# Nine of sixteen transpositions of normalized tokens move from TensorE to VectorE in an attention and mixture-of-experts kernel

## The chip, the cores and the metric

The kernel runs on one core of one Trainium2 chip. A core has engines that each run their own stream of instructions in order: TensorE (PE in the profile, with its weight loads as PEld), VectorE (DVE), ScalarE (ACT), GpSimd (POOL), and SyncE (SP), which here only issues DMAs. They work on SBUF, an on-chip memory of 128 partitions. TensorE writes its results into PSUM, a second one, of eight banks of 128 partitions x 512 f32. The metric is the device time of one execution in microseconds.

## The reference

The input x is 4096 tokens of 256 f32. One layer of a transformer is computed, all in f32:

```python
n = layernorm(x)                       # no scale, no shift
Q, K, V = n @ Qw, n @ Kw, n @ Vw
x = x + softmax(mask(Q @ K.T / 16)) @ V            # causal, one head of 256
h = layernorm(x) @ W_in + b_in
probs = softmax(h @ W_gate + b_gate)   # 8 experts
topv, topi = top_k(probs, 2); topv = topv / sum(topv)
out_e = relu(h @ W1[e] + b1[e]) @ W2[e] + b2[e]    # 256 -> 1024 -> 256
x = x + (sum over the two chosen e of topv_e * out_e) @ W_out + b_out
```

Each token goes through two of the eight experts, and only those are computed.

## The kernel before, in words

**Tokens.** The 4096 tokens are 8 blocks b of 512 (`TB`), a block is 4 tiles of 128. The whole x lies in SBUF (`xb[b]`), tokens on partitions. TensorE contracts over partitions, so whatever is multiplied by a weight matrix must first be turned, features on partitions. That is wanted twice for each block, sixteen times in all: for the first layer norm (k=0, the turned block `zT[b]` serves as keys and gives queries and values) and for the second (k=1, `z1T`, input of the experts). `ln_stats` (L214) takes mean and variance of a tile on VectorE, `ln_rstd` (L219) makes the reciprocal root of a block on GpSimd, `ln_rows` (L225) makes the shift (L229) and normalizes four tiles on VectorE (L236). `turn` (L242) turns a block: eight 128x128 transposes on TensorE into two PSUM tiles of tag `tr` (L247), each copied to SBUF by VectorE (L248).

**Attention.** It goes by half blocks of 256 queries, g = 0 to 15, with b = g // 2 and q = g % 2. `scores(g)` makes the scores transposed, keys on partitions, one piece of 256 keys x 256 queries at a time, c = 0 to g: eight matmul instructions into one of four PSUM banks of tag `mm` (L453), a copy to SBUF by ScalarE (L462) and then, on VectorE, a running elementwise maximum over the pieces (L468, "mx"). The last piece is masked (L472). The maxima are brought together in `top` (L480 to L483), turned by TensorE (`pt`, L489), reduced, and spread over all partitions (`pmax`, L496). VectorE subtracts them from every piece (L500, L506), and ScalarE takes the exponential (L503, L509). Pieces lie in 24 SBUF buffers of tag `s`. `attend(g)` multiplies the pieces by the values (`po`, L518), divides by the sum, adds to x (L528, L530) and takes the second norm's statistics. `project(b)` makes queries and values of a block (L411, L423). Qw and Kw are first multiplied into one matrix, so that the normalized tokens themselves serve as keys.

**Order.** The loop over g (L950) writes scores(g+1) ahead of attend(g). In a half g with q = 0 it normalizes block b+1 for the first norm, runs `enter(b-1)` (turn of the second norm, `ph` matmuls for h and the router, two DMAs to `rows` in DRAM on SP's queue, L275), turns block b+1, attends, projects block b+1, and runs `route(b-1)` (top two experts and each token's place, some thirty small VectorE operations, eight indirect stores to `slots` on GpSimd's queue, L341, and x += b_out on GpSimd, L360). In a half with q = 1 it ends with `ln_rstd(1, b)`, the first norm's statistics of block b+2, and the second norm's normalization of block b. In the last block's first half (g = 14) `enter(6)` is called in the middle of scores(15), at c = `BETWEEN`; then come `plan("a")`, the table of the experts' full blocks made from the first six token blocks, `route(6)`, and the first four `fetch_rows` (a slot list on SP's queue, L691, and two indirect gathers from `rows` on GpSimd's queue, L707) and three `fetch_weights` (SP's queue).

What is written in this order isn't yet the order of execution. A planner of the kernel framework runs the program ahead of time with its own prices for each instruction, and lets each engine take, of what is ready in that run, what stands first in the program. The order found so is then fixed for each engine's stream; semaphores keep it correct on the chip whatever the true durations are. Tiles of one tag share a set number of buffers, and a tile waits until a buffer is free. `tc.keep_in_program_order(ins)` adds an edge from the instruction that was written just before `ins` on the same engine, so the planner can't take `ins` ahead of it; the expert phase uses it through `pin` (L769).

**Experts.** From L1065 on, blocks of 256 or 128 token slots run through their expert: rows gathered, turned by VectorE in 32x32 squares (`squares`, L773, `STREAM_TRANSPOSE`), two matmul layers (L812 or L842, L879), results scattered to `parts`. At the end the two parts of each token are added (L1010), turned and multiplied by W_out.

Of the kernel before, what the change touches and what calls it, by code (L numbers as in the profile page):

```python
# [29 lines left out]
USUAL = 6  # L30
BETWEEN = 6
KT = VT = 8
# [3 lines left out]
def preln_attention_moe_kernel(  # L36
# [50 lines left out]
    stream = ctx.enter_context(tc.tile_pool(name="stream", bufs=1))  # L87
    dram = ctx.enter_context(tc.tile_pool(name="dram", bufs=1, space=bass.MemoryType.DRAM))
    psum = ctx.enter_context(tc.tile_pool(name="psum", bufs=1, space=bass.MemoryType.PSUM))

# [18 lines left out]

    def load_square(w, name, queue=nc.sync):  # L110
        t = const.tile([P, ND, w.shape[1]], F32, tag=name, name=name)
        queue.dma_start(out=t, in_=w.rearrange("(c p) e -> p c e", p=P))
        return t

    def load_row(v, name):
# [3 lines left out]


    kw_sb = load_square(Kw, "kw", nc.scalar)
    qw_sb = load_square(Qw, "qw", nc.scalar)
    for j in range(TPB):
# [100 lines left out]

    def ln_rows(k, b, pool):  # L225

        s = ts(b, TPB)
        mv, rstd, shift = lns[k]
        nc.vector.scalar_tensor_tensor(  # L229
            shift[:, s, :], mv[:, s, 0:1], -1.0, rstd[:, s, :], ALU.mult, ALU.mult  # L230
        )
        zs = []
        for j in range(TPB):
            t = b * TPB + j
            z = pool.tile([P, D], F32, tag=f"z{k}", name=f"z{k}_{t}", bufs=TPB)
            nc.vector.tensor_scalar(  # L236
                z, xb[b][:, j, :], rstd[:, t, :], shift[:, t, :], ALU.mult, ALU.add
            )
            zs.append(z)
        return zs  # L240

    def turn(k, b, zs, zT):  # L242

        for c in range(ND):
            pt = ps_tr(f"pz{k}_{b}_{c}")
            for j in range(TPB):
                nc.tensor.transpose(pt[:, ts(j, P)], zs[j][:, ts(c, P)], ident)  # L247
            nc.vector.tensor_copy(zT[:, c, :], pt)  # L248


# [3 lines left out]

    def enter(b, zs, pool):

        zT = pool.tile([P, ND, TB], F32, tag="z1T", name=f"z1T{b}", bufs=1)
        turn(1, b, zs, zT)
        hr = pool.tile([P, TPB, D], F32, tag="hr", name=f"hr{b}", bufs=1)

        lg = pool.tile([P, TPB, NE], F32, tag="lg", name=f"lg{b}", bufs=2)
        for j in range(TPB):
            ph = ps_mm(f"ph{b}_{j}")
            for c in range(ND):
                nc.tensor.matmul(
                    ph[:, :DG],
                    lhsT=zT[:, c, ts(j, P)],
                    rhs=win_sb[:, c, :],
                    start=(c == 0),
                    stop=(c == ND - 1),  # L270
                )
            nc.vector.tensor_tensor(lg[:, j, :], ph[:, D:DG], bgate_bc, ALU.add)
            nc.vector.tensor_tensor(hr[:, j, :], ph[:, :D], bin_bc, ALU.add)
        for k in range(TOPK):
            put = nc.sync.dma_start(  # L275
                out=rows[ts(b, TOPK * TB), :].rearrange("(t p k) d -> p t k d", p=P, k=TOPK)[
                    :, :, k, :
                ],
                in_=hr,
            )  # L280
            if b == NB - 1:
                tc.add_to_no_dep_group("last", put.ins)

        return lg
# [80 lines left out]

    attn = ctx.enter_context(tc.tile_pool(name="attn", bufs=1))

# [10 lines left out]
    def prepare_scores():  # L378

        wT = {}  # L380
        for name, w in (("qwT", qw_sb), ("kwT", kw_sb)):
            wT[name] = attn.tile([P, ND, D], F32, tag=name, name=name)
            pt = ps_tr(f"p{name}")
# [52 lines left out]

    def scores(g, between=None):


        b, q = divmod(g, QPB)  # L440
        ss, mx = [], None
        top = attn.tile([P, QB], F32, tag="top", name=f"top{g}", bufs=2)
        for c in range(g + 1):
            if between is not None and c == BETWEEN:
                between()
            ps = ps_mm(f"ps{g}_{c}")
# [14 lines left out]
            if c < g:  # L461
# [3 lines left out]
                else:  # L465
                    old = mx
                    mx = attn.tile([P, TB], F32, tag="mx", name=f"mx{g}_{c}", bufs=2)
                    nc.vector.tensor_tensor(mx, ps, old, ALU.max)  # L468
                continue
# [249 lines left out]
    def fetch_weights(item, homes=None):  # L719
        nonlocal used  # L720
        k, m = item
        parties = sets_of(item)
        sets, c2 = [], attn.tile([P, D], F32, tag="z0", name=f"c2_{k}{m}", bufs=TPB)
        es = [
# [48 lines left out]
    def squares(to, of):  # L773


        for f in range(P // SQ):
            for q in range(P // SQ):
                pin(
                    nc.vector.transpose(  # L779
                        to[ts(f, SQ)][..., ts(q, SQ)], of[ts(q, SQ)][..., ts(f, SQ)]  # L780
                    )
                )

    def turn_rows(item, h):
# [3 lines left out]
        hT = piece(f"hT_{k}{m}", ND, su * P)  # L788
        squares(
            hT.rearrange("p c (u s) -> p c u s", u=su),  # L790
            h.rearrange("p u (c f) -> p c u f", c=ND),
        )
        return hT
# [114 lines left out]
    ready = prepare_scores()  # L908
    first_rows = ln_rows(0, 0, attn)
    with tc.issue_after(ready.ins):  # L910
# [12 lines left out]
    for e in range(NE):  # L923
# [19 lines left out]
    nc.sync.dma_start(  # L943
        out=rows[TOPK * (S - TB) :, :].rearrange("(t p) d -> p t d", p=P),
        in_=zero.unsqueeze(1).to_broadcast([P, TOPK * (TPB + 1), D]),
    )

    prepare_biases()
    row = scores(0)
    for g in range(NT // KU):  # L950
        b, q = divmod(g, QPB)
        coming = q == 0 and b + 1 < NB
        lg = []

        def send():
            lg.append(enter(b - 1, rows1, attn))


        last = q == 0 and b == NB - 1
        nxt = None  # L960
        if g + 1 < NT // KU:
            nxt = scores(g + 1, send if last else None)
        if coming:
            ahead = ln_rows(0, b + 1, attn)
        if last:

            early = seen
            tables["a"] = plan("a", early, NFULL, SB, 0)
            seen = route(b - 1, lg[0], seen, attn)
            got, hTs = {}, {}  # L970
            for n in range(AHEAD + 1):
                got[n] = fetch_rows(work[n])
            for n in range(AHEAD):
                got[n] += fetch_weights(work[n])
            weighed = AHEAD
        elif q == 0 and b > 0:
            send()
        if coming:
            turn(0, b + 1, ahead, zT[b + 1])
        attend(g, row)  # L980
        row = nxt
        if coming:
            project(b + 1)
        if lg and not last:
            seen = route(b - 1, lg[0], seen, attn)
        if q == QPB - 1:
            ln_rstd(1, b)
            if b + 2 < NB:
                stats0(b + 2)
            rows1 = ln_rows(1, b, attn)  # L990

# [76 lines left out]
    for n, item in enumerate(work):  # L1068
# [21 lines left out]
        if n == 0:  # L1090
            lg = enter(NB - 1, rows1, attn)
        if n == 1:
# [70 lines left out]
```

## Time and profile before

| what | value |
|---|---|
| median of 10 runs | 1093.93 us (1093.12 to 1094.18) |
| the profiled execution | 1093.2 us, span 1091.3 us |
| TensorE busy | 1074.1 us, 98% of the span |
| VectorE busy | 692.1 us, 63% |
| ScalarE, GpSimd busy | 330.9 us, 236.9 us |
| granted TensorE clock | 1.0 throughout |
| attention ends, expert phase begins | at about 586 us |

Times are microseconds from the span's start unless ns is written. A line of a group has source line, engine, operation, output<-inputs by tile names, shapes and count, then busy time, mean duration of one in ns, idle time of the engine just before them and what ended it. A line of the timeline has start, length, engine, line, operation, and in brackets the engine's idle time before it with what released it. Matmuls are pipelined: the duration of one is longer than the distance to the next, so that costs on TensorE are read from distances between starts, not from the mean duration. An f32 matmul shows as two matmul instructions, an f32 transpose as one.

### The profile page before, as it was taken

The numbers are of one execution on the slowest core, as the hardware profiler recorded it, in microseconds if no ns is written. First come the engines' busy times: TensorE is split into PE (matmuls) and PEld (weight loads), VectorE is DVE, ScalarE is ACT, GpSimd is POOL, SyncE is SP. The second block draws the span as 40 slices with busy tenths as digits, with TensorE's granted clock in tenths as the row PEclk, the third lists the DMA queues.
The fourth block names the chain that finished last, engine by engine and source line by source line (L and its number), as shares of the span: only waits on it lengthen the run. The fifth ranks groups of instructions, "written<-read, shape, count | busy, mean of one in ns | idle before, by whom it ended". The sixth has DMA issues, their size and how long they took to land. (4 is left out here: it accounts for less than half of the span.)

```text
span 1091.3 us, 15704 instructions
## 1 busy us (share of the span) xinstructions
PE 1074.1 (98%) x5067; PEld 891.6 (82%) x5067; DVE 692.1 (63%) x2134; ACT 330.9 (30%) x727; POOL 236.9 (22%) x286
## 2 busy tenths in 40 slices
PE   7999999999999999999999999999999999999998
PEld 5768888888888888888888888786868777777887
DVE  5678576574574555446392753858678876767636
ACT  1223233332341423223132122232322332323244
POOL 2023211212001110201222332223232231313110
PEclk9999999999999999999999999999999999999999
DMA  8010101001001000100074466787979796969285
GB/s 268 1 39 1 39 2 38 2 1 40 1 1 39 1 1 1 39 1 25 16 261 160 136 189 211 252 302 245 318 237 329 242 342 209 337 216 320 92 290 192
DMA packets 114888, 148.34 MB, mean 136 GB/s; under 512 B 23149, under 2 KB 94770, under 8 KB 114804
## 3 DMA queue, kind: packets, MB, share of 16 engines
q1 hardware_dynamic: 105876, 129.70, 35.9%
q0 software_dynamic: 8384, 17.09, 4.8%
q8 instruction: 41, 0.67, 0.3%
q14 instruction: 43, 0.35, 0.2%
q10 hardware_dynamic: 544, 0.52, 0.1%
HBM read 124.79 MB, written 22.75 MB: 135 GB/s over the span
## 5 line engine op out<-in xcount | busy, mean ns | idle before, releaser
L518 PE MATMUL po<-v,s 128*128 128x257 f32 x1056 | 238.3, 380 | 0.7 <-ACT s L509 0.7
L453 PE MATMUL ps<-qT,zT 128*128 128x256 f32 x1088 | 232.8, 374 | 0.0
L453 PEld LDWEIGHTS ps<-qT,zT 128*128 128x128 f32 x1088 | 202.9, 190 | 27.1
L518 PEld LDWEIGHTS po<-v,s 128*128 128x128 f32 x1056 | 196.9, 190 | 27.7 <-issue 1.6
L462 ACT COPY s<-ps 128x512 f32<-128x512 f32 x120 | 70.2, 585 | 193.4 <-PE ps L453 154.3
L879 PE MATMUL pe_a<-w_a,mid_a 128*128 128x256 f32 x544 | 121.3, 380 | 0.0
L812 PE MATMUL pm_a<-hT_a,w_a 128*128 128x256 f32 x544 | 120.0, 379 | 0.0
L341 POOL DMA_INDIRECT slots<-assign,ati x64 | 62.6, 978 | 259.8 <-DVE ati L339 238.1
L468 DVE TENSOR_TENSOR mx<-ps,mx 128x512 f32<-128x512 f32 x91 | 62.8, 690 | 88.5 <-ACT s L462 88.0
L879 PEld LDWEIGHTS pe_a<-w_a,mid_a 128*128 128x128 f32 x544 | 102.7, 190 | 19.0 <-issue 5.6
L812 PEld LDWEIGHTS pm_a<-hT_a,w_a 128*128 128x128 f32 x544 | 103.4, 190 | 14.1
L821 ACT ACTIVATE mid_a<-pm_a,c_a 128x256 f32<-128x256 f32 x136 | 64.2, 472 | 165.6 <-PE pm_a L812 150.9
L503 ACT ACTIVATE s<-s 128x512 f32<-128x512 f32 x120 | 71.7, 629 | 51.4 <-DVE s L500 50.9
L779 DVE STREAM_TRANSPOSE hT_a<-h_a 32x128 f32<-32x128 f32 x272 | 82.2, 302 | 3.7
L500 DVE TENSOR_TENSOR s<-s,pmax 128x512 f32<-128x512 f32 x120 | 73.0, 679 | 8.2 <-PE pmax L496 8.2
L888 POOL DMA_INDIRECT parts<-y_a,slot_a x34 | 34.1, 1004 | 161.7 <-DVE y_a L887 150.8
L779 DVE STREAM_TRANSPOSE mid_c<-raw_c 32x256 f32<-32x256 f32 x128 | 55.8, 436 | 1.9
L879 PE MATMUL pe_b<-w_b,mid_b 128*128 128x256 f32 x256 | 56.8, 380 | 0.0
L812 PE MATMUL pm_b<-hT_b,w_b 128*128 128x256 f32 x256 | 56.6, 379 | 0.0
L879 PEld LDWEIGHTS pe_b<-w_b,mid_b 128*128 128x128 f32 x256 | 48.5, 190 | 9.4 <-issue 2.6
L812 PEld LDWEIGHTS pm_b<-hT_b,w_b 128*128 128x128 f32 x256 | 48.6, 190 | 6.6
L821 ACT ACTIVATE mid_b<-pm_b,c_b 128x256 f32<-128x256 f32 x64 | 30.1, 470 | 63.0 <-PE pm_b L812 63.0
(276 smaller groups left out, 1200.3 us busy)
## 6 DMA issues: line engine op xcount, KB each, us to landing
w_a<-in_L_ffn_W_dram SPq DMA_DIRECT2D x68, 512.0 KB, 5.7
w_d<-in_L_ffn_W_dram SPq DMA_DIRECT2D x48, 512.0 KB, 6.8
w_c<-in_L_ffn_W_dram SPq DMA_DIRECT2D x32, 512.0 KB, 7.9
w_b<-in_L_ffn_W_dram SPq DMA_DIRECT2D x32, 512.0 KB, 6.6
rows<-hr SPq DMA_DIRECT2D x16, 512.0 KB, 3.0
yp<-parts SPq DMA_DIRECT2D x14, 512.0 KB, 8.9
x<-in_L_attn_x_dram SPq DMA_DIRECT2D x7, 512.0 KB, 7.0
out_dram<-ot SPq DMA_DIRECT2D x14, 256.0 KB, 6.0
```

Source lines behind the costliest of these rows:

```text
L341: put = nc.gpsimd.indirect_dma_start(out=slots, out_offset=bass.IndirectOffsetOnAxis(ap=ati[:, j : j + 1], axis=0), in_=assign[:, b * TPB ...
L453: nc.tensor.matmul(ps[:, u * QB + lo : (u + 1) * QB], lhsT=zT[kt // TPB][:, d, ts(kt % TPB, P)], rhs=qT[b][:, d, q * QB + lo : (q + 1) * Q ...
L462: nc.scalar.copy(flat, ps)
L468: nc.vector.tensor_tensor(mx, ps, old, ALU.max)
L500: nc.vector.tensor_tensor(s, s, pm[:, :QB].unsqueeze(1).to_broadcast([P, KU, QB]), ALU.subtract)
L503: nc.scalar.activation(s, s, AF.Exp)
L518: nc.tensor.matmul(po[u][:, : D + 1], lhsT=ss[c][:, k, ts(u, P)], rhs=vb[kt // TPB][:, kt % TPB, :], start=(kt == 0), stop=(kt == g * KU + u),
L779: nc.vector.transpose(to[ts(f, SQ)][..., ts(q, SQ)], of[ts(q, SQ)][..., ts(f, SQ)])
L812: nc.tensor.matmul(pm[:, :SB], lhsT=w1[c][:, ts(f, P)], rhs=hT[:, c, :], start=(c == 0), stop=(c == ND - 1),)
L821: nc.scalar.activation(mid[f // 2][:, f % 2, :], pm[:, :SB], AF.Relu, bias=c1[:, f : f + 1])
L879: nc.tensor.matmul(pe[ts(j, rest), :D], lhsT=mid[f][:, ts(u, P)][:, ts(j, rest)], rhs=w2[f // (NF // 2)][:, f % (NF // 2), :], start=(f == 0),
L888: put = nc.gpsimd.indirect_dma_start(out=parts, out_offset=bass.IndirectOffsetOnAxis(ap=slot[:, u : u + 1], axis=0), in_=y[:, u, :], in_of ...
```

## The change

`TURNED = (4, 2)` takes the place of `BETWEEN = 6`. Blocks from 4 on of the first norm (4, 5, 6, 7) and blocks 2 to 6 of the second are no longer turned by TensorE but by VectorE, nine of sixteen. For such a block `ln_rows` returns its work as a list (`fill`) in place of doing it: one shift, four normalizations, and from `rows_todo` sixteen transposes, each of 32 partitions x 256 elements. The next call of `scores` takes the list, and puts equal parts of it behind its running maxima c = 1 to g-1, each instruction tied to the one before by `keep_in_program_order`. So the first norm's block b+2 is turned in scores(2b+2), g = 6, 8, 10, 12, and the second norm's block b in scores(2b+3), g = 7, 9, 11, 13, 15.

To that end the first norm's statistics and normalization of block b+2 move from the end of half q = 1 to the end of half q = 0, behind `route`, for all blocks. `enter` no longer turns. In half g = 14 `enter(6)` leaves the middle of scores(15); the table and the four `fetch_rows` come ahead of it and `route(6)` behind attend(14). Since rows are then fetched before blocks 6 and 7 have entered, the zeros that are stored in `rows` at the start reach over both blocks. The four normalized tiles of a block are one tile with one buffer (`z0`, `z1`), and Kw, Qw, their turned copies and later the rows of b2 share one tag (`sq`) with four buffers.

```diff
-BETWEEN = 6
+TURNED = (4, 2)
+    def square(name):
+        return attn.tile([P, ND, D], F32, tag="sq", name=name, bufs=4)
-    def ln_rows(k, b, pool):
+    def ln_rows(k, b, fill=None):
...
+        todo = [shifts] + [partial(normalize, j) for j in range(TPB)]
+        if fill is None:
+            for do in todo:
+                do()
+        else:
+            fill += todo
+        return z
+    def squares_todo(to, of):
+        return [
+            partial(nc.vector.transpose, to[ts(f, SQ)][..., ts(q, SQ)], of[ts(q, SQ)][..., ts(f, SQ)])
+            for f in range(P // SQ)
+            for q in range(P // SQ)
+        ]
+    def rows_todo(hT, h):
+        return squares_todo(
+            hT.rearrange("p c (u s) -> p c u s", s=P), h.rearrange("p u (c f) -> p c u f", f=P)
+        )
-    def scores(g, between=None):
+    def scores(g, fill=()):
+        parts_of = max(g - 1, 1)
...
-                    nc.vector.tensor_tensor(mx, ps, old, ALU.max)
+                    done = nc.vector.tensor_tensor(mx, ps, old, ALU.max)
+                    for do in fill[len(fill) * (c - 1) // parts_of : len(fill) * c // parts_of]:
+                        tc.keep_in_program_order(done)
+                        done = do()
+                    if fill:
+                        tc.keep_in_program_order(done)
...
-        out=rows[TOPK * (S - TB) :, :].rearrange("(t p) d -> p t d", p=P),
-        in_=zero.unsqueeze(1).to_broadcast([P, TOPK * (TPB + 1), D]),
+        out=rows[TOPK * (S - LATE * TB) :, :].rearrange("(t p) d -> p t d", p=P),
+        in_=zero.unsqueeze(1).to_broadcast([P, TOPK * (LATE * TPB + 1), D]),
...
     row = scores(0)
+    ahead = ln_rows(0, 1)
+    fill = []
     for g in range(NT // KU):
...
-            nxt = scores(g + 1, send if last else None)
+            nxt = scores(g + 1, fill)
+        fill = []
+        if q == 0:
+            if b == NB - 1:
+                early = seen
+                tables["a"] = plan("a", early, NFULL, SB, 0)
+                got, hTs = {}, {}
+                for n in range(AHEAD + 1):
+                    got[n] = fetch_rows(work[n])
+            if b > 0:
+                if b - 1 < TURNED[1]:
+                    turn(1, b - 1, rows1, z1T)
+                lg = enter(b - 1, z1T, attn)
+            if b == NB - 1:
+                for n in range(AHEAD):
+                    got[n] += fetch_weights(work[n])
+                weighed = AHEAD
+            elif b + 1 < TURNED[0]:
+                turn(0, b + 1, ahead, zT[b + 1])
         attend(g, row)
         row = nxt
-        if coming:
+        if q == 0 and b + 1 < NB:
             project(b + 1)
-        if lg and not last:
-            seen = route(b - 1, lg[0], seen, attn)
+        if lg is not None:
+            seen = route(b - 1, lg, seen, attn)
+        if q == 0 and b + 2 < NB:
+            stats0(b + 2)
+            by_dve = b + 2 >= TURNED[0]
+            ahead = ln_rows(0, b + 2, fill if by_dve else None)
+            if by_dve:
+                fill += rows_todo(zT[b + 2], ahead)
         if q == QPB - 1:
             ln_rstd(1, b)
-            if b + 2 < NB:
-                stats0(b + 2)
-            rows1 = ln_rows(1, b, attn)
+            z1T = attn.tile([P, ND, TB], F32, tag="z1T", name=f"z1T{b}", bufs=1)
+            by_dve = TURNED[1] <= b < NB - 1
+            rows1 = ln_rows(1, b, fill if by_dve else None)
+            if by_dve:
+                fill += rows_todo(z1T, rows1)
```

## The prediction

> **What bounds the kernel now.** First the page: engine totals, then the slices.
>
> ```profile
> PE 1074.1 (98%) x5067; PEld 891.6 (82%) x5067; DVE 692.1 (63%) x2134; ACT 330.9 (30%) x727; POOL 236.9 (22%) x286
> DVE  5678576574574555446392753858678876767636
> ```
>
> TensorE is busy 98% of the span, so time is gained only by taking work from it, and lost by any hole put into it. VectorE has room, unevenly. Then busy time by stretch (columns PE, PEld, DVE, ACT, POOL) tells where TensorE still idles:
>
> ```profile
> 27.00:64.00 37.00, 32.48 (x159) 25.80 (x157) 26.56 (x76) 10.78 (x27) 5.02 (x5) 1.00 0.00 1
> 64.00:124.00 60.00, 59.23 (x279) 48.01 (x276) 45.12 (x155) 15.56 (x35) 12.95 (x13) 1.00 0.11 36
> 124.00:184.00 60.00, 60.00 (x286) 50.86 (x286) 40.30 (x118) 18.61 (x37) 12.81 (x13) 1.00 0.06 18
> 443.00:586.00 143.00, 142.71 (x667) 122.87 (x666) 75.13 (x218) 37.56 (x69) 26.86 (x27) 1.00 0.22 72
> ```
>
> From 124 us on there is no hole. Each new one is paid in full. Next the groups, for prices:
>
> ```profile
> L247 PE MATMUL pz<-ident,z 128*128 128x128 f32 x128 | 17.8, 273 | 1.8 <-DVE s L506 1.8
> L248 DVE COPY z1T<-pz 128x512 f32<-128x512 f32 x16 | 10.9, 686 | 14.6 <-PE pz L247 14.4
> L779 DVE STREAM_TRANSPOSE hT_a<-h_a 32x128 f32<-32x128 f32 x272 | 82.2, 302 | 3.7
> L779 DVE STREAM_TRANSPOSE mid_c<-raw_c 32x256 f32<-32x256 f32 x128 | 55.8, 436 | 1.9
> ```
>
> Last the timeline around scores(6) (124.07 to 139), with two earlier lines where TensorE waited for VectorE:
>
> ```profile
> 59.04 0.33 PE L489 MATMUL pt<-ident,top 128*128 128x128 f32 x1 [1.51 <-DVE top L481]
> 104.12 0.65 PE L489 MATMUL pt<-ident,top 128*128 128x128 f32 x2 [0.42 <-DVE top L481]
> 114.21 1.04 PE L247 MATMUL pz<-ident,z 128*128 128x128 f32 x8
> 115.08 1.90 PE L518 MATMUL po<-v,s 128*128 128x257 f32 x8
> 124.07 11.91 PE L453 MATMUL ps<-qT,zT 128*128 128x256 f32 x56
> 137.56 0.42 PE L489 MATMUL pt<-ident,top 128*128 128x128 f32 x2
> ```
> ```profile
> 56.38 2.00 DVE L480 TENSOR_TENSOR top<-mx 128x256 f32<-128x256 f32 x1
> 130.19 0.69 DVE L468 TENSOR_TENSOR mx<-ps,mx 128x512 f32<-128x512 f32 x1 [1.08 <-ACT s L462]
> 136.85 0.41 DVE L481 TENSOR_TENSOR top<-top,s 128x256 f32<-128x256 f32 x1
> 609.42 4.40 DVE L779 STREAM_TRANSPOSE hT_a<-h_a 32x128 f32<-32x128 f32 x14
> 613.85 0.42 DVE L887 TENSOR_TENSOR y_a<-pe_a,c_a 128x256 f32<-128x256 f32 x1
> ```
>
> A score piece takes TensorE 1.73 us (eight matmuls, 216 ns apart); VectorE spends 0.69 on its maximum and idles about 1.04. That hole is what the change fills. The top of scores(6) is there at 136.85+0.41 = 137.26 and its turn pt starts at 137.56: the fixed order meets the maxima with 0.3 us to spare. Where VectorE was later than planned, TensorE stood (1.51 and 0.42).
>
> **What the change takes from TensorE.** A turn's eight transposes run from 114.21 to 115.08, 0.87 us (109 ns each; the 273 of the group is overlapping duration). Nine turns: **-7.8 us**, all on the path. Here a rule of the Trainium skill speaks against the change: "VectorE: DVE Perf Modes", sections "The three transpose paths" and "Rules for kernel authors", advises TensorE for a whole 128x128 turn and prices it at 390 ns there. By its figure the nine turns would free 72 x 0.39 = 28 us, an estimate from that page for another data type; the trace's 109 ns stands.
>
> **What it gives VectorE.** Off: 18 copies of 0.686, 12 us. On: 144 transposes of 32x256, 436 ns long, which follow one another about 14 ns apart (in the 32x128 row, 4.40/14 = 314 against 302): 0.45 each, 65 us. A fill is 16 x 0.45 = 7.2, plus the shift (0.2) and four normalizations (0.345 apart) that move in: 8.8 us over g-1 parts in scores(g), g = 6 to 13 and 15. Per part: 1.76 (g=6), 1.46, 1.25, 1.10, 0.97 (g=10), down to 0.63. From g=10 it fits the 1.04 hole. For g = 6 to 9 the maxima slip by 0.72, 0.42, 0.21, 0.06 a part, at most 2.9 us at the last maximum. TensorE may run ahead of a maximum by four banks: 3 x 1.73 less copy and maximum (0.585+0.69) leaves 3.9 us, so the slip alone doesn't stop it. Behind the last maximum, its part and the 1.2 us chain to top (136.02 to 137.26) are late too; attend(g-1) is there to fill that, 10.4 us at g=6, if the order places it. The edges themselves add one wait: a fill's first maximum stands behind the last VectorE instruction of the iteration before, a statistic that is out by then; 0. Behind a fill item that waits stand all later maxima, the masks and top, and behind these, by banks or by pt, TensorE.
>
> **Does the order know?** The order is fixed by a planner with its own prices, and the trace shows one being low. Expert block 0 puts out y_a at 609.08 and 613.85; the second is released by 16 matmuls after the first, 16 x 0.217 = 3.47 us, and comes earlier in the program than the transposes. On the chip 7 of these fit before it; the planner put 14. So it counts at most (3.47-0.42)/13 = 0.235 for what takes 0.314. With the 134 ns that 128 more elements cost (436-302), a 32x256 is planned at 0.37 or less against 0.45. Then pt, or for the second norm the first ph, is placed too early. At 0.37 the lateness that isn't planned is 16 x 0.08 = 1.25 us for g = 6, 7, 8, where VectorE is the slower one at either price, 0.94 for 9, where holes take up some of it, and only the last part's, 0.26 or less, from 10 on. Less the 0.3 to spare: 3 x 0.95 + 0.64 = **+3.5**. Ends: 0 if the planner's price is right; 6.8 (same working) if it plans 0.30, what the shorter 32x128 takes. I take 3.5, the value that the order of y_a gives.
>
> **The collisions with GpSimd.** x<-x,bout (2.35 us) held the SBUF-to-SBUF maximum at 56.38 for 2.00 us where its kind takes 0.53, and cost the 1.51 above. In the blocks that TensorE still turns, the first norm's shift and normalizations leave scores(3) and scores(5), where both waits were, for the project before; the collision stays. Between 0 and -1.9: **-0.7**. In the fills of the second norm it can hold a shift or normalization 2 us; only g=7 and 9 have no hole for it. Between 0 and +4: **+0.5**, since GpSimd is free for it right after rstd and mostly done when the pinned shift comes.
>
> **The rest.** Waits of pq and ph for turned copies go: 0 to -0.9, **-0.3**. stats0(b+2) and its two GpSimd operations move ahead of the second half of block b; their price is in the rival below. Merged z tiles and kw, qw, turned weights and b2 rows sharing one tag: the same number of slots, and turn(0,b+1) ends long before the next normalization; 0. The zero store grows from 10 to 18 tiles of 128 KB, 1.05 MB, 4 us of DMA at the 268 GB/s of the first slice; behind it on SP's queue the next store is hr at 68 us; 0. At the end of attention four slot loads on SP and eight gathers (1.26 us apart, 10 us of GpSimd) go ahead of block 6's enter and route; its two row stores then wait for the gathers on SP's queue, weights queue behind these, and its eight slot stores come 25 us later. The cover is attend(14) and attend(15), 54 us of TensorE; weights now leave at 546 and are first used at 586. If that cover were short, lateness would be paid up to some 2 us; enter(6) in the middle of scores(15) costs no hole to undo (0.3 idle in 443 to 586): **0**.
>
> Sum: -7.8+3.5-0.7+0.5-0.3 = **-4.8 us** on the profiled execution: 1093.2 (span 1091.3) becomes 1088.4. The runs' median, 1093.93, is 0.7 above it: **1089.1**.
>
> **Rivals.**
> *All hidden.* The planner's price is right for this shape, or TensorE arrives later than I think: -8.8, 1085.1. For it: no wait for pt from 124 us on. Against it: the 14 transposes ahead of y_a.
> *Given back whole.* Planned price of 0.27 to 0.30 and one or two collisions: 6 to 10 us back, 1091.7 to 1096, no measurable change. For it: the 0.235 is an upper bound. Against it: VectorE idles whole microseconds elsewhere.
> *Slower: the shift behind the slot stores.* rstd of the next first norm must now pass GpSimd near route's eight slot stores. In block 2 they start at 125.40; behind them rstd would end 8 x 1.26 + 1.3 later, 136.8, while the pinned shift is due at 129.1 and every maximum stands behind it. 7.7 late less 3.9 of banks leaves 3.8 us of TensorE for each of four fills, 15 us: 1104. It decides from about 6 us late a fill. For it: statistics come last in the program. Against: attend's statistics already interleave with route's small operations, which leaves them done by about 124.
>
> **How the numbers follow.** What this kernel's measurement tells from no change is about 0.2%, 2.2 us. The forecast (2 to 6 given back, 1086.5 to 1091.5) 0.45; all hidden 0.20; given back whole 0.19; slower 0.16. Faster 0.65, same 0.19, slower 0.16. The range goes from the all-hidden end, 1085, to 1097: it leaves out the far part of the slower case and a sliver below.
>
> **What would show it.** L247 down to 56 transposes and a new 32x256 transpose group of 144 near 436 ns; TensorE's busy share unchanged; waits of pt or ph for VectorE of about a microsecond at scores(6) to (9), few later. Wrong if TensorE shows holes inside the score pieces (banks), if shift waits for rstd on GpSimd, or if pt doesn't wait at all.

## The result and the profile after

| | before | after |
|---|---|---|
| median | 1093.91 us | 1103.49 us (8 runs, 1100.52 to 1104.14) |
| ratio | | 1.0085, interval 1.0076 to 1.0094 |
| profiled execution, span | 1093.2, 1091.3 us | 1102.56, 1100.8 us |
| TensorE busy, idle within the span | 1074.1, 17.2 us | 1072.6, 28.2 us |

The change costs 9.6 us; 4.8 us of gain were forecast. The page of the changed kernel, engine totals and TensorE's row of slices:

```profile
PE 1072.6 (97%) x4995; PEld 887.4 (81%) x4995; DVE 734.1 (67%) x2260; ACT 331.3 (30%) x727; POOL 236.8 (22%) x286
...
PE   7999999999999999999989999999999999999998
```

VectorE has 42 us more: the turns less the dropped copies make 50.4, and five shifts of the first norm give 9.6 back. Before, these five took 2.08 us each, from 97.38 to 99.47 us for one, while GpSimd's x += b_out ran from 97.09 to 99.44; now every shift of the first norm takes 0.15 or 0.16. TensorE's totals hardly move, and one slice of its row falls from 9 to 8. The busy time by stretch (columns PE, PEld, DVE, ACT, POOL, granted clock, DMA share, GB/s) says where it now idles:

```profile
27.00:64.00 37.00, 33.69 (x163) 26.71 (x162) 26.82 (x76) 11.39 (x27) 4.89 (x5) 1.00 0.03 5
...
124.00:184.00 60.00, 55.46 (x249) 46.56 (x248) 48.16 (x138) 17.22 (x33) 11.44 (x11) 0.97 0.06 18
184.00:256.00 72.00, 69.16 (x324) 59.20 (x323) 53.29 (x145) 23.19 (x45) 12.79 (x13) 1.00 0.05 15
...
443.00:586.00 143.00, 138.83 (x635) 118.46 (x634) 81.52 (x232) 37.66 (x69) 26.98 (x27) 0.99 0.23 58
```

Where TensorE had been busy for 60.00 of 60, it is busy for 55.46; in the stretch at the end of attention 4.2 us are idle, where 0.3 were. The clock, 1.00 everywhere before, is 0.97 and 0.99 in two of these rows. The groups, shapes kept apart, show that the change itself did what it says:

```profile
L495 DVE STREAM_TRANSPOSE z1T<-z 32x256 f32<-32x256 f32 x80 | 34.9, 436 | 1.7
L495 DVE STREAM_TRANSPOSE zT<-z 32x256 f32<-32x256 f32 x64 | 27.9, 436 | 1.3
...
L261 PE MATMUL pz<-ident,z 128*128 128x128 f32 x56 | 8.5, 291 | 1.0 <-DVE s L535 1.0
```

144 turns of 436 ns on VectorE, 56 transposes left on TensorE. Counted from start to start, the transposes take 9.0 us of TensorE's time in place of 16.4. The list of TensorE's waits (total, times, longest) names three that are new or grown; before, pt had 1.9 us, ph 0.2, and pk was not listed:

```profile
PE pt L518 <- DVE top L510: 5.5, 4, 2.2
PE ph L290 <- DVE z1T L495: 4.5, 5, 2.4
PE pk L348 <- DVE both L339: 4.2, 2, 3.9
```

The first two are one kind, seen in the timeline of scores(6), VectorE and then TensorE, and in that of scores(7):

```profile
128.00 0.69 DVE L492 TENSOR_TENSOR mx<-ps,s 128x512 f32<-128x512 f32 x1 [3.21 <-ACT s L486]
...
130.91 1.32 DVE L495 STREAM_TRANSPOSE zT<-z 32x256 f32<-32x256 f32 x3
...
135.52 1.79 DVE L495 STREAM_TRANSPOSE zT<-z 32x256 f32<-32x256 f32 x4
137.34 0.69 DVE L492 TENSOR_TENSOR mx<-ps,mx 128x512 f32<-128x512 f32 x1
138.07 2.25 DVE L495 STREAM_TRANSPOSE zT<-z 32x256 f32<-32x256 f32 x5
...
141.18 0.42 DVE L510 TENSOR_TENSOR top<-top,s 128x256 f32<-128x256 f32 x1
```
```profile
123.64 11.91 PE L477 MATMUL ps<-qT,zT 128*128 128x256 f32 x56
135.39 4.07 PE L547 MATMUL po<-v,s 128*128 128x257 f32 x18
141.65 0.66 PE L518 MATMUL pt<-ident,top 128*128 128x128 f32 x2 [2.18 <-DVE top L510]
...
167.77 1.57 PE L290 MATMUL ph<-win,z1T 128*128 128x264 f32 x6 [2.36 <-DVE z1T L495]
```

VectorE idles for 3.21 us ahead of the first maximum, and then has five turns left behind the last one, directly ahead of `top`, which comes 4.3 us later than before (141.18 against 136.85; counted from the start of the scores, 17.5 against 12.8, 4.8 later). TensorE was given 18 instructions of attend to fill that; they end 2.2 us too early. The third wait lies at the end of attention, TensorE and then VectorE:

```profile
544.70 1.57 PE L290 MATMUL ph<-win,z1T 128*128 128x264 f32 x6 [0.30 <-DVE z1T L495]
...
548.90 13.18 PE L547 MATMUL po<-v,s 128*128 128x257 f32 x60
565.95 0.45 PE L348 MATMUL pk<-both,before 128*128 128x32 f32 x2 [3.87 <-DVE both L339]
```
```profile
543.66 0.89 DVE L495 STREAM_TRANSPOSE z1T<-z 32x256 f32<-32x256 f32 x2
...
547.76 9.05 DVE L529 TENSOR_TENSOR s<-s,pmax 128x512 f32<-128x512 f32 x15 [0.17 <-PE pmax L525]
...
558.08 0.17 DVE L324 TENSOR_REDUCE best<-lg 128x4 f32<-128x32 f32 x1
...
565.62 0.18 DVE L339 TENSOR_TENSOR both<-hot,hot 128x32 f32<-128x32 f32 x1
```

Before, the same ph were:

```profile
511.11 3.83 PE L265 MATMUL ph<-win,z1T 128*128 128x264 f32 x16 [0.22 <-DVE z1T L248]
```

Block 6's last turn now ends at 544.55, so the ph of enter(6) run at 544.7, where they ran at 511.1. Their evictions are thus caught on both sides of VectorE's nine-microsecond run of subtractions, and route(6) starts only at 558.08. The matmul pk, placed behind sixty instructions of attend, waits for it 3.87 us with the rest of attend(15) behind it.

Counted from start to start, less each line's usual distance, the holes ahead of pt and ph from 60 us on add up to 10.8 us (1.8 before), and the one ahead of pk at the end of attention is 4.0. The largest at pt and ph are 2.34, 2.52, 1.75 and 1.42, in scores(6) to (9). Behind the 2.34 and the 4.0 the clock is halved for 3.41 us, at 142.87 and at 566.12, and each such stretch costs about 1.6 us more.

### The profile page after: what moved, and what is told of

Same layout as the page of the kernel before. It is cut to its first block, busy times and chain, and to the rows that moved or that the text cites. A ratio compares the mean times of both kernels' runs of the same rounds, so it can differ in the third digit from the quotient of the medians.

```text
span 1100.8 us, 15686 instructions
## 1 busy us (share of the span) xinstructions
PE 1072.6 (97%) x4995; PEld 887.4 (81%) x4995; DVE 734.1 (67%) x2260; ACT 331.3 (30%) x727; POOL 236.8 (22%) x286
## 5 line engine op out<-in xcount | busy, mean ns | idle before, releaser
L547 PEld LDWEIGHTS po<-v,s 128*128 128x128 f32 x1056 | 200.0, 192 | 28.5 <-issue 0.8
L532 ACT ACTIVATE s<-s 128x512 f32<-128x512 f32 x120 | 71.7, 629 | 50.9 <-DVE s L529 50.4
```

What stands on the lines that cost most here:

```text
L532: nc.scalar.activation(s, s, AF.Exp)
L547: nc.tensor.matmul(po[u][:, : D + 1], lhsT=ss[c][:, k, ts(u, P)], rhs=vb[kt // TPB][:, kt % TPB, :], start=(kt == 0), stop=(kt == g * KU + u),
```

## The experiments

Each kernel is the changed one with the edit shown. Times are medians, and ratios are to the kernel before as measured in the same set; it took 1093.8 to 1094.1 us in three of the four sets.

**First set: which part of the change, and is it VectorE's room or TensorE's order?** The first theory put the waits at pt and ph on TensorE's fixed order (the planner counts a turn too low), and the wait at pk on the early table, whose experts' turns share VectorE with route(6).

`all_pe`, all nine turns back on TensorE, the moved steps kept:

```diff
-TURNED = (4, 2)
+TURNED = (8, 7)
```

> The change with TURNED = (8, 7): TensorE turns all sixteen blocks again, every other part of the change stays. Theory (the planner prices a VectorE transpose too low, so what TensorE does behind a chain with transposes is placed too early): the waits of pt and ph from 124 us on, 10 us, and the half-clock stretch behind the first of them, 1.7 us, go; nine turns come back, 7.6 us; the wait of pk at 562 us with its half-clock stretch, 5.8 us, stays, since the experts' transposes that stand in route(6)'s way stay: 1103.5 - 11.8 + 7.6 = 1099.3. Rival (the moved steps, earlier statistics and normalizations, later enter(6) and route(6), cost the time): the waits of pt and ph stay and the turns come on top, about 1111.

Measured: 1105.83 us, ratio 1.0109 (1.0092 to 1.0126), between the two expectations. The waits at pt and ph go, as the theory said. The end of attention gets worse:

```profile
553.41 3.73 PE L290 MATMUL ph<-win,z1T 128*128 128x264 f32 x16
...
565.05 1.19 PE L833 MATMUL pm_a<-hT_a,w_a 128*128 128x256 f32 x2 [7.48 <-issue]
566.03 0.51 PE L348 MATMUL pk<-both,before 128*128 128x32 f32 x2
```

A matmul of the experts stands ahead of pk and waits 7.48 us (the rows that it reads are turned by 564.94), and 13.65 us at half clock around it cost some 4.2. So the moved steps alone, without any VectorE turn, cost about 12 us.

`held`, the first `HELD[g+1]` pieces of attend(g) (`first`) written in scores(g+1) ahead of pt, so that TensorE has that work there whatever the planner thinks; turns and edges stay:

```diff
+HELD = {6: 4, 7: 4, 8: 3, 9: 3, 10: 2, 11: 2, 12: 2, 13: 2}
...
+        if first is not None:
+            first()
         for u in range(KU):
-            nc.tensor.transpose(pt[:, ts(u, P)], top[:, ts(u, P)], ident)
+            turned = nc.tensor.transpose(pt[:, ts(u, P)], top[:, ts(u, P)], ident)
+            if first is not None and u == 0:
+                tc.keep_in_program_order(turned)
...
```

> The change, with the first pieces of attend(g) written into scores(g+1) ahead of pt, and pt tied behind the last of them by one edge: 4 pieces (6.9 us) at scores(6) and (7), 3 at (8) and (9), 2 at (10) to (13). VectorE's work is untouched. Theory (placed too early): the waits of pt and ph fall from 10 us to under 2 and the half-clock stretch at 143 us goes; the pk wait stays: 1103.5 - 11 = about 1092.5. Rival (capacity: with the fill VectorE is late by more than TensorE has work for): the wait only moves to another place, 1101 or more.

Measured: 1091.4 us, 0.9977 (0.9967 to 0.9986). The timeline of scores(6):

```profile
122.81 11.91 PE L478 MATMUL ps<-qT,zT 128*128 128x256 f32 x56
134.56 7.11 PE L556 MATMUL po<-v,s 128*128 128x257 f32 x32
141.51 0.38 PE L521 MATMUL pt<-ident,top 128*128 128x128 f32 x2
```

32 instructions ahead of pt in place of 18, and no wait. VectorE does the same work as in the changed kernel, so its capacity was not the fault; the work that TensorE could have done was there. The hole at pk stays (4.0 us).

`routed`, the experts' first three turn steps held behind route(6)'s last counting operation, and `held_routed`, both edits:

```diff
...
-    for n in range(AHEAD):
-        hTs[n] = turn_rows(work[n], got[n][1])
+    with tc.issue_after(counted[NB - 2].ins):
+        for n in range(AHEAD):
+            hTs[n] = turn_rows(work[n], got[n][1])
```

> The change, with the transposes of the first three expert blocks issued on VectorE only behind the last counting step of route(6) (one issue-order edge each). Theory: these transposes stand between route(6)'s small operations, each 0.1 us longer than planned, and pk waits 3.9 us for the counts; with the edges pk's wait and the half-clock stretch behind it go, 5.8 us: 1097.7, and no hole appears at the experts' start, since 15 us of transposes end by 580 and the first expert matmul is at 595. Rival (route(6) is late because enter(6) and its stores stand behind the fetches): pk waits as before, 1103.5.

> Both edits of held and routed. Theory: both losses go and the nine turns' 7.8 us remain as gain: about 1086.5, under the kernel before. Rival (the loss comes back as another wait once VectorE is full): 1092 or more.

Measured: 1097.98 us, 1.0037 (1.0023 to 1.0051), and 1086.02 us, 0.9927 (0.991 to 0.9943), both as expected. The hole at pk shrinks from 4.0 to 1.4, and no half clock follows it. `held_routed` beats both kernels, the one before by 7.9 us.

**Second set.** Here the kernel before itself took 1106.0 us, for a reason that no run shows, and all four traces have a wait at the first expert blocks that the traces of no other set have, with half clock behind it. So these runs are read against the kernel before of the same set, and not to a microsecond. The line from one of them (TensorE's waits, `late_fills_routed`):

```profile
PE pm_a L837 <- ACT mid_a L846: 6.4, 1, 6.4
```

`all_pe_routed` is `all_pe` with `routed`; `deeper` is `held_routed` with `TURNED = (3, 1)` and held pieces for two fills more; `late_fills_routed` is `routed` with `TURNED = (6, 4)`; `no_edges` leaves out the edges of the whole list, so that the shift and the normalizations are free too:

```diff
                     for do in fill[len(fill) * (c - 1) // parts_of : len(fill) * c // parts_of]:
-                        tc.keep_in_program_order(done)
-                        done = do()
-                    if fill:
-                        tc.keep_in_program_order(done)
+                        do()
```

> All nine turns go back to TensorE (no VectorE turn of a fill), the other moved steps stay, and the first three turn steps of the experts' tokens wait for route(6)'s last counting operation. Theory (the fault of the moved steps is only that the experts' turns share VectorE with route(6)'s chain): the hole ahead of pk and the half clock behind it, 7.6 + 4.6 = 12.2 us in the run with all turns on TensorE, go: 1105.8 - 12.2 = 1093.6, so within 1 us of the kernel before, 1093 to 1095. Rival (the moved fetch and table cost something by themselves): 1097 or more.

> The kernel with the held pieces and the held route, with VectorE turns in two fills more, eleven in all (from the run of 4 on), and held pieces there too. Theory (the turns pay while VectorE's own work fits beside TensorE's): two turns more are worth 2 x 0.87 = 1.7 us, but in scores(4) VectorE needs 4 running maxima of 1.09 us, pieces of the shift and five turns of 1.8 us, some 16.4 us, beside 14.7 us of TensorE, so about 2 us come back as a wait at pt or ph of scores(4): 1086.0 - 1.7 + 2 = 1086.3, range 1085 to 1088. If all of it is hidden: 1084.3. Rival (VectorE is full from there on and the lateness is handed from fill to fill): 1089 or more.

> The changed kernel without the edges that hold the nine turns in program order behind the running maxima. Theory (the lateness at pt and ph comes of the low planned price of the turns, not of the edges): waits at pt and ph of scores(6) to (9) of about the same total, some 8 to 10 us, and the hole ahead of pk as before: 1101 to 1105. Rival (the edges make the lateness, since they keep a running maximum and a turn from changing places): 1098 or less.

> VectorE turns in five fills only, from the longer ones on, and the held route; no held pieces. Theory (in the long fills VectorE has the room, and the lateness is some 0.4 to 0.7 us a fill there): 5 x 0.87 = 4.3 us less for TensorE, some 2 us of waits at pt and ph back, nothing at pk: 1093.9 - 4.3 + 2 = 1091.6, range 1090.5 to 1093. Rival (a turn on VectorE costs as much as it saves wherever it is put): 1094 or more.

Measured: 1111.94 us, ratio 1.005 (1.0031 to 1.0069); 1102.69, 0.9964 (0.9952 to 0.9975); 1108.46, 1.0016 (1.0005 to 1.0027); 1108.55, 1.0019 (1.0009 to 1.0029). All four end on the rival's side. `late_fills_routed` has a hole of 1.9 us at pt of scores(6), where it has no VectorE turn, so part of this belongs to the set and not to the edit. But `all_pe_routed` keeps a hole of 4.1 us at pk with the experts' turns out of the way, which the early table can't explain. Its ph come at 556.6.

**Third set: both theories again.** `late_table_pe` (all turns on TensorE) and `late_table_held` (with the held pieces) take the early table away; `no_edges_again` and `after_again` are `no_edges` and the changed kernel itself side by side.

```diff
-            if b == NB - 1:
-                early = seen
-                tables["a"] = plan("a", early, NFULL, SB, 0)
-                got, hTs = {}, {}
-                for n in range(AHEAD + 1):
-                    got[n] = fetch_rows(work[n])
...
         if lg is not None:
+            early = seen
             seen = route(b - 1, lg, seen, attn)
+        if q == 0 and b == NB - 1:
+            tables["a"] = plan("a", early, NFULL, SB, 0)
+            got, hTs = {}, {}
+            for n in range(AHEAD + 1):
+                got[n] = fetch_rows(work[n])
+            for n in range(AHEAD):
+                got[n] += fetch_weights(work[n])
...
```

> All nine turns on TensorE, and the first table, its gathers and the first weights come behind route(6), at the end of the iteration of attend(14), in place of ahead of enter(6). Theory (the hole at the end of attention comes from the early table: the experts' first turns are ready while route(6)'s chain runs, and VectorE's order takes them one for one): the 12.2 us of hole and half clock in the run with all turns on TensorE go, 1105.8 - 12.2 = 1093.6, so the time of the kernel before, 1092.5 to 1095. Rival (route(6) itself, now behind attend(14), has too little TensorE work ahead of its pk, whoever else is on VectorE): a wait of 3 to 4 us at pk stays, with a half clock behind it, 1098 or more.

> Held pieces as before, nine turns on VectorE, and the first table, its gathers and the first weights behind route(6); no edge on the experts' turns. Theory (early table at fault): like the run with held pieces and held route, 1085.5 to 1087.5. Rival (route(6) itself has too little ahead of it): the hole of 4 us and its half clock stay, 1090 or more.

> The changed kernel without the edges, a second time, now beside the changed kernel itself on one chip. In its first run TensorE's holes at pt and ph were 7.6 us (10.4 in the changed kernel), and the one at pk 1.3 (4.0). Theory now (the low planned price makes the lateness, and the edges make it larger, since without them the planner may let a maximum pass a turn): 3 + 3 us below the changed kernel, so 1096 to 1099 beside 1103.5. Rival (the edges change nothing, the difference was the other chip's): within 2 us of the changed kernel.

> The changed kernel itself, unedited, for the comparison on one chip: 1100.5 to 1104.2 where the kernel before takes 1093.9, and 9 to 10 us above the kernel before on any chip.

Measured: `late_table_pe` 1103.36 us, 1.0088 (1.0071 to 1.0105), on the rival's side. With no experts' turn on VectorE near route(6), pk still waits:

```profile
553.19 3.73 PE L290 MATMUL ph<-win,z1T 128*128 128x264 f32 x16
...
561.29 0.61 PE L348 MATMUL pk<-both,before 128*128 128x32 f32 x2 [3.94 <-DVE both L339]
```

`late_table_held` 1088.99, 0.9957 (0.9941 to 0.9974), between the two expectations: the hole at pk is the 1.4 of `held_routed`, and the later rows bring 1.0 at the first pm_a and 1.4 at block 7's turn. `after_again` 1103.33, 1.0084 (1.0067 to 1.0101). `no_edges_again` 1091.05, 0.9974 (0.9964 to 0.9985): 12.3 us below the changed kernel, twice what was expected. Leaving out the edges closes most of both kinds of hole. VectorE's timeline in scores(6), and TensorE's pt:

```profile
127.56 3.58 DVE L494 STREAM_TRANSPOSE zT<-z 32x256 f32<-32x256 f32 x8
131.16 0.69 DVE L492 TENSOR_TENSOR mx<-ps,s 128x512 f32<-128x512 f32 x1
...
133.98 0.89 DVE L494 STREAM_TRANSPOSE zT<-z 32x256 f32<-32x256 f32 x2
...
134.97 2.28 DVE L492 TENSOR_TENSOR mx<-ps,mx 128x512 f32<-128x512 f32 x3
```
```profile
136.86 1.90 PE L544 MATMUL po<-v,s 128*128 128x257 f32 x8
138.60 0.51 PE L515 MATMUL pt<-ident,top 128*128 128x128 f32 x2
```

Eleven of the sixteen turns now run ahead of the first maximum, for the most part in time that VectorE had idle (the first maximum starts 6.05 us behind the first matmul of the scores, where it was 4.36), and the last ends at 134.87; three maxima follow without a break, and pt doesn't wait. The turns are the same and as long as before; they only no longer stand between the last maxima and `top`. The planner's order on TensorE is another too, with eight instructions of attend ahead of pt in place of 18. The holes at pt and ph are 3.3 us in place of 10.8. And block 6's turns end at about 512 in place of 544.5, the ph run at 533 to 539, and `both` is ready at 545.1, with the subtractions behind it:

```profile
544.95 0.19 DVE L339 TENSOR_TENSOR both<-hot,hot 128x32 f32<-128x32 f32 x1
545.06 9.05 DVE L526 TENSOR_TENSOR s<-s,pmax 128x512 f32<-128x512 f32 x15
```
```profile
555.85 0.38 PE L348 MATMUL pk<-both,before 128*128 128x32 f32 x2
```

The hole at pk is 0.3 us, and 0.8 more stand at the matmul behind it.

**Fourth set: the edges by halves.** `last_free` keeps the edges in scores(6) to (13) and leaves them out in the last fill, `last_edged` the other way round (`==` in place of `<`).

```diff
-                        tc.keep_in_program_order(done)
+                        if g < NT // KU - 1:
+                            tc.keep_in_program_order(done)
                         done = do()
-                    if fill:
+                    if fill and g < NT // KU - 1:
                         tc.keep_in_program_order(done)
```

> The changed kernel, with the edges in the fills of scores(6) to (13) and none in the last fill, that of scores(15). Theory (the edges of the last fill spread block 6's turns to the end of scores(15), 514 to 544 in the changed kernel, so that enter(6) and route(6) fall behind the subtraction of the maxima, and pk finds route(6) unfinished): the turns end by about 515, the hole of 4.0 us at pk and the one or two half-clock stretches behind it (1.7 each) go, the holes at pt and ph stay: 1103.3 - 3.7 - 1.7 to 3.4 = 1096 to 1098. Rival (the early table makes that hole): 1101 or more.

> The other half: no edges in the fills of scores(6) to (13), edges in that of scores(15). Theory: the holes at pt and ph stay small (some 2 us above the kernel before), the hole of 4 us at pk is back, with its half clock: 1091.0 + 3.7 + 1.7 to 3.4 = 1096.5 to 1098. Rival (the early table, or the early edges, make the hole at pk): 1093 or less, or 1101 or more.

Measured: 1097.91 us, 1.0035 (1.0023 to 1.0048), as expected, and 1096.13, 1.0021 (1.0011 to 1.0031), 0.4 below the theory's range and far from the rival's; TensorE's waits, first of `last_free`, then of `last_edged`:

```profile
PE pt L519 <- DVE top L511: 5.5, 4, 2.2
PE ph L290 <- DVE z1T L496: 4.2, 4, 2.4
```
```profile
PE pk L348 <- DVE both L339: 4.2, 2, 3.9
PE pt L519 <- DVE top L511: 1.9, 3, 1.2
PE ph L290 <- DVE z1T L496: 1.9, 2, 1.6
```

| | edges in scores(6) to (13) | none there |
|---|---|---|
| edges in scores(15) | 1103.3: pt and ph 10.8, pk 4.0 | 1096.1: pt and ph 3.7, pk 4.0 |
| none there | 1097.9: pt and ph 10.4, pk 0.3 | 1091.05: pt and ph 3.3, pk 0.3 |

(Holes in us from start to start. 1103.3 and 1091.05 are of the third set, the other two of the fourth, where the kernel before was 0.3 us slower. The 0.8 us behind pk come on top in the lower row.) The two halves add: 5.4 and 7.2 alone, 12.3 together. The table is early in all four, so it doesn't make the hole at pk by itself; with the nine turns on VectorE, the edges of the last fill do.

`no_edges_held` joins the two remedies, `no_edges_held_deeper` adds `TURNED = (3, 1)` and held pieces for two fills more.

> No edges on the turns, and the first pieces of attend(g) written in scores(g+1) ahead of pt. Theory (what is left without edges is TensorE's order at pt and ph of scores(7), 1.6 + 0.7 us, because the planner's price of a turn is low): these holes close, 1091.0 - 2.3 = 1088.7, range 1086 to 1090. Rival (the held pieces help only against the edges): 1090.5 or more.

> As no_edges_held, with VectorE's turns in two fills more, those of scores(4) and scores(5), eleven turns. Theory (VectorE has room for them as long as their place is free): 2 x 0.87 = 1.7 us less, of which some is lost in scores(4), where VectorE needs about 16.4 us beside 14.7 of TensorE: 1086.5 to 1089, 0 to 1.7 below the kernel with nine. Rival (VectorE is full in scores(4) and (5)): slower than with nine by 1 us or more.

Measured: 1088.69 us, 0.9949 (0.9932 to 0.9965), and 1089.54, 0.9958 (0.9941 to 0.9974). The first is as expected. The second misses its range by 0.5: two turns more save 1.7, and holes of 2.7 us are new ahead of pk (1.4), pt (0.9) and pmax (0.4). The new holes lie between 111 and 129 us, behind the fill of scores(5). That VectorE has no room there, as `deeper` suggested, is a reading of this; no run tested it. `held_routed`, 1086.02, stays the best.

## Why the prediction was wrong

**What was right.** TensorE's gain, forecast at 7.8, is 7.4 (the nine turns are worth 7.8; the very first turn, at 11.8 us, now takes 0.46 longer). The turns take the 436 ns forecast. The holes are where it put them: at pt and ph of scores(6) to (9), 8.0 of the 10.8, with little later; none lies inside the score pieces. Against its scores `top` of scores(6) slipped by 4.8 us, where the slip and last part came to 4.7. The slower rival's mechanism did not happen, though the time ended beside its 1104: GpSimd's `rstd` is out at 122.9, ahead of the first slot store at 124.98, and the shift runs at 128.61, directly behind its maximum. The collisions in the fills, +0.5, did not come: all normalizations of the second norm took 403 to 414 ns. The early waits shrank by 1.2 (TensorE idle between 27 and 64 us: 4.5, now 3.3), within the 0 to 1.9 given for -0.7. (The maximum that was held for 2.00 us is of a kind that takes 0.41 in that trace, not 0.53.)

**First wrong step: "Does the order know?", +3.5, ends 0 and 6.8.** It measured 9.1 (10.84 less the 1.75 of before), beyond the far end. If the hole is put on the sixteen turns, it is 2.34/16 = 0.15 in scores(6) and 2.52/16 = 0.16 in scores(7), and with the 0.3 us that pt had to spare a little more: an estimated planned price of 0.27 to 0.30, where the trace has 0.45 and the working took 0.37. The 0.37, from the order of y_a, was an upper bound, and the sum took the bound as the value. (A slip in the sum hardly matters: by the working's own figures the lateness of scores(9) is 7 x 0.06 + 1.10 - 0.94, about 0.6 and not 0.94, which makes 3.1 of the 3.5.) That the price is low fits the numbers; no run changed the price itself. What the runs show is that the price alone is not enough. The prediction took the place of the turns as given, and asked only how far they make the maxima late. Without the edges the same turns, at the same price, cost 3.3 us of holes, because most of them run in VectorE's idle time ahead of the first maximum; with the edges that time (3.21 us in scores(6)) is closed to them, and the last part stands on the path to `top`. The edges were costed at "one wait ... 0".

**Second wrong step: "The rest", 0, up to some 2 us.** The hole measured 4.0, and about 1.6 more behind it at half clock (twice that in `after_again`, whose stretch is 6.83 us long). The step looked at TensorE's load around enter(6) ("costs no hole to undo") and at queues and DMAs, and found cover in attend(14) and (15). It did not ask when enter(6)'s input is ready: the last fill's equal parts reach to the end of scores(15), 544 us, and with it route(6) falls behind VectorE's subtractions. `all_pe` and `late_table_pe` reach the same late ph (553) by another way, since there block 6's turn on TensorE comes late, and have a hole of at least 4 us too. The early table fell as the cause by itself; it shares in the hole when route(6) is late, since holding back the experts' turns takes 2.6 of the 4.0 (`routed`). No run put `enter(6)` back into the middle of scores(15), so what that move costs by itself stays open.

**Put at nothing: the half clock.** The sum has no term for it. The profiled run has two stretches, 3.3 us together.

The account on the profiled execution: -7.4 for the turns, +9.1 at pt and ph, +4.0 at pk, +3.3 at half clock, -1.2 early: +7.8 of the 9.5 by which the span grew. The remaining 1.7 us lie in small differences of distance that were not followed up.

## What to carry to other kernels

An instruction that is tied behind others to keep it out of the way also loses the idle time ahead of them: see first where the engine idles, and what the last of the tied pieces stands in front of. When work is moved to another engine, ask for every consumer when its input is now ready, and what long run on that engine comes next, and not only whether the other engine has cover. Where an order is fixed ahead of time by estimated prices, give the waiting engine work by program order at the point where the estimate is doubtful: pieces held ahead of pt turned a loss of 9.6 us into a gain of 2.5, and with the second hole treated too, of 7.9.

## What the runs showed of the hardware

A short hole on TensorE can cost nearly twice its length. In the changed kernel the half-clock stretches begin at 142.87 and 566.12 us, 423.25 apart, which is 124 times 3.4133; in every trace the changes of the clock lie on such a grid, and the stretches are 3.41, 6.83, 10.24 or 13.65 long. The Trainium skill, "TensorE: Matmul & The Clock Gate", Part 1, section "What's actually happening", describes a free-running window of 3413 ns that doesn't start with the kernel; these traces agree. Laying the stretches of the grid over the profile (the columns are those of the busy time by stretch), first the changed kernel, then `last_free`:

```profile
139.46:142.87 3.41, 1.23 (x7) 0.94 (x7) 2.81 (x8) 0.27 (x1) 0.00 (x0) 1.00 0.00 0
142.87:146.28 3.41, 3.41 (x11) 2.69 (x10) 2.47 (x5) 1.69 (x3) 0.00 (x0) 0.50 0.00 0
163.35:166.77 3.42, 2.06 (x11) 1.49 (x10) 3.27 (x8) 0.00 (x0) 0.00 (x0) 1.00 0.00 0
166.77:170.18 3.41, 2.41 (x11) 1.94 (x12) 3.22 (x11) 0.27 (x1) 0.00 (x0) 1.00 0.00 0
```
```profile
137.41:140.82 3.41, 2.57 (x12) 1.90 (x10) 3.29 (x7) 0.00 (x0) 0.00 (x0) 1.00 0.00 0
140.82:144.24 3.42, 2.09 (x11) 1.69 (x12) 2.27 (x7) 0.27 (x1) 0.00 (x0) 1.00 0.00 0
144.24:147.65 3.41, 3.41 (x18) 2.98 (x17) 3.41 (x7) 2.94 (x5) 0.00 (x0) 1.00 0.00 0
```

A hole of 2.2 us that falls into one window leaves 1.23 us of work in it, and the next window runs at half clock, 11 instructions in place of 18. The 2.4 us ahead of ph in scores(7) are split over two windows, and nothing follows. In `last_free` the very same hole at pt of scores(6), 2.17 us, falls across a boundary and costs only itself. So whether a hole of this size is paid twice depends on where the grid lies in that execution. From 60 us on, whole windows with 2.2 us idle or more always began such a stretch, and outside the second set windows with 1.9 or less never did. In `no_edges` of the second set, windows with 1.82 and 1.63 us idle did, so there is no sharp bound between the two, and what else counts stays open. The same page's section "Why this matters for your kernels" asks for no idle gaps over about 3 us; here 2.2 us were enough, and the measurement decides.

It also fits the scatter of the changed kernel's runs, 3.6 us, where 28 runs of the kernel before lie within 1.6: at a mean clock of 0.998 it took 1100.52, at 0.997 1102.56 to 1102.69, at 0.995 1103.02 to 1104.14 (mean 1103.64). The steps, 2.1 and 1.0 us, are of the size of the 1.6 that one such window costs.
